# Layer norm applied to gathered rows, means and squares of attention's sums from a weight column and ScalarE, weight sums on GpSimd, and last choices of 12 and 8 tiles

## The chip, the cores and the metric

One core of one Trainium2 chip runs the whole kernel in a single launch. The metric is the device time in microseconds (us) of an execution. Times of a kernel are given as the median of several runs; a profile is one execution of its own, whose time is given beside its span.

In the profile PE is TensorE's matrix product, PEld its weight load, DVE is VectorE, ACT ScalarE, POOL GpSimd, and SP the engine that starts most transfers. L12 is line 12 of the kernel before.

## The reference, cut to what matters

The model has three blocks, each after a layer norm without gain: a mixture of experts, attention, the same mixture of experts again. x is (4, 2048, 256), so N = 8192 tokens of D = 256.

```python
x = x + 0.5 * moe(layernorm(x), router_w, wg, wu, wd)
x = x + attention(layernorm(x), Wq, bq, Wv, bv, Wo, bo)
x = x + 0.5 * moe(layernorm(x), router_w, wg, wu, wd)

def attention(x):                      # 16 heads of 16
    q, v = heads(x @ Wq + bq), heads(x @ Wv + bv)
    q = softmax(q, over the 16 columns of a head) * s
    k = softmax(q, over the tokens) * s          # keys are made of q
    return merge(q @ (k.T @ v)) @ Wo + bo

def moe(x):                            # 8 experts, F = 1024
    topw, topi = top_k(softmax(x @ router_w.T), 2)
    topw = topw / (topw.sum() + 1e-6)
    # every expert takes the 1280 tokens with the largest weights among those that chose it
    eo = (silu(rows @ wg[e]) * (rows @ wu[e])) @ wd[e]
    return scatter_add(topw * eo)
```

The layer norm is (x - mean) / sqrt(var + 1e-5) over the 256 columns. As the norm has no gain, it is one factor and one addend for each token: x * rstd + shift, with rstd = 1/sqrt(var + 1e-5) and shift = -mean * rstd.

## The kernel before, in words

The tokens are 64 tiles (T) of 128 (P). They lie in SBUF as xw, 128 x 64 x W: W = D + 2E = 272 columns (L61), of which the first 256 are the token's row of x and the 16 behind them are used for the router. Everything is float32 on TensorE. All arithmetic of PE, DVE, ACT and POOL runs on each engine in the order in which it is written (`manual_schedule`; in the stage of the experts POOL's is left out of it); the transfers that SP starts (`write_rows`, the stores of the output, the loads of weights) have an order of their own.

**First router** (`first_router`, L1178). Per quad of tiles, rows are transposed and multiplied with the router's weights, whose column means have been taken away, so that no mean of x is needed for the logits. DVE's bn_stats give mean and variance of a row in two halves; `norm_of` (L171) makes rstd and shift of them with four DVE operations, `deviation` (L165, POOL, two operations) and three more on POOL. Then `choose` (L212) finds the two best experts of every token with their renormalised weights: some twenty small DVE operations and one exp on ACT, as a generator that stops eleven times, and at the end two POOL operations that write, into the 16 columns behind a row, half the weight for each expert (L272) and whether the expert was chosen (L273). The weights also go to w.

**Route** (`route`, L278). For each expert the 1280th largest weight is found by 30 steps of bisection on the bits of a float. A step is a compare on DVE that also counts (L309), a small product on TensorE that adds the counts over the partitions (L310), and three small DVE operations, the last at L316; the next compare needs the result. Equal weights are settled after it (L322 to L336), running counts become slots (scans at L328 and L337, L338), four transposes bring them back to the order of the tokens (L343), and L345 to L353 split the slots in two parts. `next(beside, None)` (L311) lets another generator issue a few instructions in every step. In the first route that is `norm_beside` (L198): it normalises the 64 tiles in place, by turns on POOL (L194) and ACT (L196), writes them tile by tile of 16 to DRAM (`write_rows`, L275), and drives `attention_weights` (L861), which prepares the weights of attention with some small products. In the second route nothing runs beside.

**Experts** (`experts`, L452; 16 chunks of five tiles, two chunks for each expert). `RowList` (L355) makes the list of an expert's 1280 tokens by one-hot products (L413); its end, L427, yields the indices ixs (L433). `gather` (L464) fetches the rows of a chunk with an indirect DMA for each tile (L471, POOL), 272 columns wide. `blank` (L477) multiplies each row with the column that says whether the token chose this expert, since slots that no token fills hold another token's row. `turn` transposes the rows (L496), and the products follow. Gate and up products use a seven-product scheme (Strassen-Winograd): it needs sums of the weights' blocks, ws (`sums_of_w`, L507: eight DVE operations of 128 x 512 for each expert, recorded at L502) and wds (`sum_of_wd`, L520, four DVE operations), and sums of the rows' blocks (`sums_of_x`, L544). `sixth_product` (L610) ends in the DVE addition u2. Results are scaled by the token's weight (L703) and added to DRAM by indirect DMA (L704). At the start of the stage (L835 to L851) the order on DVE is: ixs, the eight sums ws of expert 0, then the odd tile's blank; in chunk 0 `sum_of_wd(0)` stands ahead of the sixth product (L635).

**Attention** (`attention`, L924). The tiles are taken two at a time (i = 0 to 31) through a software pipeline, one iteration of the loop at L1123 for each pair: `stats` (L938), `turn_x`, `project` (L957: q, and with 8 columns more the router's logits of x), `largest` (L962), `exp` (L975), `share` (L979 to L982), `keys` (L989, L991), `turn_q` (L1000), `sums` (L1012, the product of keys and x, summed over a batch element of 8 pairs). After a batch element `context_1` to `context_4` (L1021 to L1062) make the matrix that turns q into attention's output and, in 8 further columns, into its part of the next router's logits: W1 = D + E = 264 columns (L857). Then `add_y` (L1064) multiplies, and `take_y` (L1078) adds the result to the row (L1080), takes bn_stats of the two tiles (L1082), starts the store of four tiles to the output (L1085), and every second time calls `norm_of`. When 16, 16, 12, 16 and 4 tiles are complete (L1091), a `choose` is started for them, and `choose_on` (L1097) drives it: two steps in each iteration, with two `norm_row` on ACT, until the choice is through and its rows are written. The loop's tail, from L1165 on, has its own counts of steps; the last two choices run side by side from L1170 on, and their rows are normed after them (L1173).

In each iteration the written order on ACT is xs and ek of pair i-3 (`keys`), exp of pair i-2, the copies of the two transposes, and then what `choose_on` and `take_y` issue.

Of the kernel before, what the change touches and what calls it, by code (L numbers as in the profile page):

```python
# [1 line left out]

# [24 lines left out]
def macaron_kernel(  # L27
# [33 lines left out]
    W = D + 2 * E  # L61
# [128 lines left out]
    def norm_row(xw, t, gpsimd=False):  # L190

        row, by, of = xw[:, t, 0:D], rstd[:, t : t + 1], shift[:, t : t + 1]
        if gpsimd:
            nc.gpsimd.tensor_scalar(row, row, by, of, ALU.mult, ALU.add)  # L194
        else:
            nc.scalar.activation(row, row, AF.Identity, bias=of, scale=by)  # L196

    def norm_beside(xw, to, steps=iter(())):  # L198


        t, busy = 0, True
        while t < T or busy:
            busy = next(steps, 0) != 0
            for gpsimd in (True, False) if busy else (False, True, False):
                if t < T:
                    norm_row(xw, t, gpsimd)
                    t += 1
                    if t % NJ == 0:
                        write_rows(xw, to, slice(t - NJ, t))
            yield  # L210

    def choose(xw, w, ts, pool):  # L212
# [60 lines left out]
        nc.gpsimd.tensor_scalar(xw[:, ts, D + E :], by_token, 0.0, None, ALU.is_gt)  # L273
# [4 lines left out]
    def route(w, pool, ppool, beside=iter(())):  # L278
# [5 lines left out]
        def new(name):  # L284
            return pool.tile(FULL, F32, name=name)
# [17 lines left out]
        above, tie = new("above"), new("tie")  # L303
# [36 lines left out]

        ps = ppool.tile([P, GT, P], F32, tag="turn", name="back", bufs=1)
# [110 lines left out]
    def experts(name, src, dst, wait_for, weights, wpool, pool, ppool):  # L452
# [8 lines left out]
        lists, got, xTs, turned, ws, wds, xs = {}, {}, {}, {}, {}, {}, {}  # L461
# [15 lines left out]
        def blank(k, *tiles):  # L477
            for i in tiles:
                if k < len(chunks):
                    e, r = chunks[k][0], got[k][i]  # L480
                    has = r[:, D + E + e : D + E + e + 1]
                    if k == 0 and i % 2:
                        nc.vector.tensor_scalar(r[:, 0:D], r[:, 0:D], has, None, ALU.mult)
                    else:
                        nc.scalar.mul(r[:, 0:D], r[:, 0:D], has)
# [21 lines left out]
        def sums_of_w(e, m):  # L507

            if e >= E:
                return  # L510
            if m == 0:
                ws[e] = pool.tile([P, 2, 4, FH], F32, tag="ws", name="ws", bufs=1)
            v, o = weights[e][m], ws[e]
            a11, a12, a21, a22 = v[:, 0, :FH], v[:, 1, :FH], v[:, 0, FH:], v[:, 1, FH:]
            tt(o[:, m, 0, :], a21, a22, ALU.add)
            tt(o[:, m, 1, :], o[:, m, 0, :], a11, ALU.subtract)
            tt(o[:, m, 2, :], a11, a21, ALU.subtract)
            tt(o[:, m, 3, :], a12, o[:, m, 1, :], ALU.subtract)
# [40 lines left out]
        def units(k):  # L559
# [75 lines left out]
            sum_of_wd(k, 0)  # L635
            sixth_product(0)
            sum_of_wd(k, 1)
# [92 lines left out]
        def early(k, p):  # L730

            if p == 0 and more:
                lists[chunks[k][0] + 1] = more.pop(0).end()
                gather(k + 1)
            elif p == 2:
                blank(k + 1, 0, 1, 2, 3)
            elif p == 3:
                blank(k + 1, 4)
# [97 lines left out]
        with tc.manual_schedule(engines=ENGINES - {mybir.EngineType.Pool}):  # L836
# [9 lines left out]
            for m in range(2):  # L846
                sums_of_w(0, m)
            blank(0, *range(TURN))
            for q in (0, 2):
                turn(0, q)  # L850
            blank(0, *range(TURN, CH))  # L851
# [5 lines left out]
    W1 = D + E  # L857
# [3 lines left out]
    def attention_weights(pool, ppool):  # L861
# [21 lines left out]
        nc.gpsimd.tensor_copy(wqx[:, :, D:], wrx[:, :, :E])  # L883
# [20 lines left out]
        for k in range(DC):  # L904
            for c in range(DC):
                nc.tensor.matmul(
                    ps[:, k * E : (k + 1) * E], woT[:, c, k * P : (k + 1) * P], wqx[:, c, D:],
# [3 lines left out]
        nc.scalar.copy(wox[:, :, D:], ps[:, : DC * E].rearrange("p (k e) -> p k e", k=DC))  # L911
        yield
        ps = ppool.tile([P, 2 * D], F32, tag="turn", name="bor", bufs=1)
        for c in range(DC):
            bob = pool.tile([P, P], F32, tag="bob", name="bob", bufs=2)
            nc.scalar.mul(bob, ones, boT[:, c : c + 1])
            nc.tensor.matmul(ps[:, :E], bob, wqx[:, c, D:], start=(c == 0), stop=(c == DC - 1))
            yield
        nc.scalar.mul(box[:, D:], ps[:, :E], 1.0 / H)
# [4 lines left out]
    def attention(xw, w, to, weights, pool, ppool):  # L924
# [6 lines left out]
        st3 = pool.tile([P, T, 6], F32, name="st3")  # L931
# [144 lines left out]
        choosing, chosen = [], []  # L1076

        def take_y(i, ps):  # L1078
            xs = xw[:, 2 * i : 2 * i + 2, 0:W1]
            nc.vector.tensor_tensor(xs, xs, ps[:, :, 0:W1], ALU.add)  # L1080
            for t in (2 * i, 2 * i + 1):
                nc.vector.bn_stats(st3[:, t, :], xw[:, t, 0:D])  # L1082
# [3 lines left out]
            if i % 2:  # L1086
                norm_of(st3, slice(2 * i - 2, 2 * i + 2), pool)
# [3 lines left out]
            for n in (NJ, NJ, NJ - 4, NJ, 4):  # L1091
                stop += n
                if 2 * i + 2 == stop:
                    ts = slice(stop - n, stop)
                    choosing.append((ts, choose(xw, w, ts, pool), list(range(ts.start, stop))))

        def choose_on(n, m, which=0):  # L1097

            while len(choosing) > which and n:
                ts, steps, tiles = choosing[which]  # L1100
                while n:
                    n -= 1
                    if next(steps, 0) == 0:
                        steps = None
                        break
                if steps is None and ts.stop > T - NJ:
                    chosen.append(choosing.pop(which))
                    continue
                for t in tiles[: m if steps else None]:
                    norm_row(xw, t)  # L1110
                del tiles[:m]
                if steps is None:
# [7 lines left out]
        with tc.manual_schedule(engines=ENGINES):  # L1120
            stay_busy(ppool.tile([P, 2, 2 * D], F32, tag="py", name="py", bufs=1)[:, 0, :], 7)
            stats(0, 2)
            for i in range(LAST):  # L1123
# [6 lines left out]
                if b3 == B - 1:  # L1130
                    choose_on(1, 0)
# [192 lines left out]
```

## Time and profile before

| | |
|---|---|
| median of three runs | 1992.24 us (1991.15 to 1992.62) |
| the profiled execution's own time | 1991.06 us |
| its span | 1989.1 us |
| mean granted TensorE clock | 0.959 |
| busy PE | 1831.6 us (92%), 8756 products |
| busy PEld | 1332.4 us |
| busy DVE, ACT, POOL | 1401.2, 957.6, 1019.5 us |
| moved by DMA | 147.66 MB |

The span divides into stages, by the times of their first and last instructions:

| stage | us |
|---|---|
| first router and its choice | 0 to 49 |
| first route, bisection from 50.6 to 90.7 | 49 to 103 |
| list of expert 0, gather, start of the products | 103 to 127 |
| experts | 127 to 895 |
| attention, with the choices for the second experts | 895 to 1136 |
| second route, list and start | 1136 to 1213 |
| experts | 1213 to 1989 |

The lines shown in the prediction are of two kinds. A stretch has its bounds (A:B), its length, and then the busy time of PE, PEld, DVE, ACT and POOL with the number of instructions that began in it, the granted clock as a share of full speed, the busy share of the DMA engines, and GB/s. A line of the instructions in order of time has start, duration, engine, line, operation, result and operands with their shapes; in brackets stands how long the engine was idle before it, and what ended that.

### The profile page before, as it was taken

To read this page: it belongs to the slowest core of one execution; us is meant where nothing else is said; L and a number is where in the kernel's file an instruction comes from. 1 tells how busy PE (TensorE), PEld (TensorE's weight loads), DVE (VectorE), ACT (ScalarE), POOL (GpSimd) and SP (SyncE) were. 2 spreads that over 40 slices of the span, in tenths; PEclk is the share of its full clock that TensorE was granted. 3 is DMA by queue.
4 is the path that set the end of the run, shared out by engine and by line. 5 is a ranking of instruction groups with operands and counts; after the bars stand their busy time and mean duration, and the time that the engine had idled before them with its cause. 6 is when DMAs were issued, how large, how long until landed. Compare 5 with 4: busy or idle time off the path is not lost.

```text
span 1989.1 us, 25375 instructions
## 1 busy us (share of the span) xinstructions
PE 1831.6 (92%) x8756; PEld 1332.4 (67%) x8756; DVE 1401.2 (70%) x2555; ACT 957.6 (48%) x2371; POOL 1019.5 (51%) x1017
## 2 busy tenths in 40 slices
PE   6379999999999999999999627999999999999997
PEld 5247777777777777777887415777777777777776
DVE  7866767676767676647788886676767676676763
ACT  5435454554546463325565405554646363737332
POOL 4435555555555555535555304555555555555552
PEclk8589999999999999999999858999999999999999
DMA  9911313222222221125002531222222222231121
GB/s 357 309 29 28 91 31 88 58 61 71 49 70 49 71 49 28 28 24 172 33 33 88 191 135 29 67 52 71 49 70 49 70 49 75 44 94 29 31 29 19
DMA packets 99935, 147.66 MB, mean 74 GB/s; under 512 B 7512, under 2 KB 86368, under 8 KB 99680
## 3 DMA queue, kind: packets, MB, share of 16 engines
q1 hardware_dynamic: 69072, 102.77, 15.2%
q0 software_dynamic: 30720, 43.27, 13.4%
q8 instruction: 69, 1.13, 0.2%
q14 instruction: 58, 0.48, 0.1%
q10 hardware_dynamic: 16, 0.01, 0.0%
HBM read 98.84 MB, written 55.57 MB: 78 GB/s over the span
## 4 chain that ended last, share of the span: by engine, by line
PE 82%; DVE 8%; issue 1%; POOL 1%; ACT 1%; DMA 1%; POOLq 0%; DVEq 0%; ACTq 0%; SPq 0%
PE mm L570 48%; PE mm L770 23%; PE tr L496 2%; PE back L722 2%; PE qp L957 1%; PE pc L1012 1%; PE ix L413 1%; PE py L1070 1%; DVE above L309 1%; PE mm L828 1%; DVE st L1082 1%; DVE xw L1080 1%; DVE q L965 1%; DVE m L970 0%; DVE z L979 0%
## 5 line engine op out<-in xcount | busy, mean ns | idle before, releaser
L570 PE MATMUL mm<-xs,ws 128*128 128x320 f32 x1536 | 476.9, 433 | 3.9 <-DVE u L502 3.0
L505 POOL TENSOR_TENSOR ct<-ct 128x320 f32<-128x320 f32 x360 | 338.8, 941 | 190.2 <-DVE ct L601 166.7
L570 PEld LDWEIGHTS mm<-xs,ws 128*128 128x128 f32 x1536 | 284.3, 190 | 113.0 <-DVE u L502 4.1
L502 DVE TENSOR_TENSOR ct<-u,mm 128x640 f32<-128x640 f32 x256 | 209.8, 819 | 180.1 <-PE mm L570 169.0
L502 DVE TENSOR_TENSOR ct<-ct,mm 128x640 f32<-128x640 f32 x288 | 235.8, 819 | 74.6 <-PE mm L570 74.1
L598 ACT ACTIVATE ct<-ct 128x960 f32<-128x960 f32 (+2 forms) x192 | 141.7, 738 | 298.7 <-DVE ct L502 298.7
L471 POOL DMA_INDIRECT r<-rows,ixs x160 | 157.6, 985 | 235.9 <-ACT eo L703 172.8
L770 PE MATMUL mm<-ct,wds 128*128 128x320 f32 x960 | 278.5, 433 | 0.0
L407 ACT ACTIVATE lo<-from_below,behind_lo 128x129 f16<-128x129 f32 x896 | 272.9, 395 | 0.0
L770 PEld LDWEIGHTS mm<-ct,wds 128*128 128x128 f32 x960 | 178.5, 190 | 73.2 <-DVE ct L502 6.4
L770 PE MATMUL mm<-ct,wdt 128*128 128x320 f32 x720 | 213.5, 433 | 0.0
L704 POOL DMA_INDIRECT acc<-eo,ixs x80 | 127.7, 1596 | 141.9 <-ACT eo L703 124.0
L704 POOL DMA_INDIRECT out_dram<-eo,ixs x80 | 127.6, 1596 | 141.9 <-ACT eo L703 124.0
L570 PE MATMUL mm<-xsT,wgt 128*128 128x320 f32 x512 | 183.5, 440 | 0.0
L570 PE MATMUL mm<-xsT,wut 128*128 128x320 f32 x512 | 180.7, 435 | 0.0
L601 DVE TENSOR_TENSOR ct<-ct 128x640 f32<-128x640 f32 (+1 forms) x128 | 166.0, 1297 | 18.8 <-ACT ct L598 18.8
L502 DVE TENSOR_TENSOR u<-p,mm 128x640 f32<-128x640 f32 x128 | 105.0, 821 | 88.3 <-PE mm L570 80.6
L770 PEld LDWEIGHTS mm<-ct,wdt 128*128 128x128 f32 x720 | 132.1, 190 | 47.5
L607 ACT COPY p<-mm 128x640 f32<-128x640 f32 x128 | 88.3, 690 | 154.3 <-PE mm L570 154.3
L570 PE MATMUL mm<-xsT,ws 128*128 128x320 f32 x512 | 158.7, 432 | 0.0
L703 ACT ACTIVATE eo<-back,r 128x256 f32<-128x256 f32 x150 | 65.0, 478 | 152.7 <-PE back L722 152.7
L570 PEld LDWEIGHTS mm<-xsT,wut 128*128 128x128 f32 x512 | 97.7, 191 | 40.7 <-issue 0.8
(226 smaller groups left out, 2820.0 us busy)
## 6 DMA issues: line engine op xcount, KB each, us to landing
wgt<-in_L_ffn_wg_dram SPq DMA_DIRECT2D x16, 1024.0 KB, 5.0
wut<-in_L_ffn_wu_dram SPq DMA_DIRECT2D x16, 1024.0 KB, 7.5
wdt<-in_L_ffn_wd_dram SPq DMA_DIRECT2D x16, 1024.0 KB, 5.3
rows<-xw SPq DMA_DIRECT2D x7, 2176.0 KB, 15.0
xw<-in_L_attn_x_dram SPq DMA_DIRECT2D x16, 512.0 KB, 8.4
out_dram<-xw SPq DMA_DIRECT2D x16, 512.0 KB, 2.9
xw<-acc SPq DMA_DIRECT2D x15, 512.0 KB, 8.8
r<-rows,ixs POOLq DMA_INDIRECT x160, 2.8
```

Source lines behind the costliest of these rows:

```text
L407: nc.scalar.activation(lo[:, t, :], from_below, AF.Sign, bias=at, scale=1.0)
L471: nc.gpsimd.indirect_dma_start(out=r, out_offset=None, in_=src[:, :], in_offset=bass.IndirectOffsetOnAxis(ap=lists[e][:, i : i + 1], axis=0),)
L496: nc.tensor.transpose(ps[:, (i - i0) * P : (i - i0 + 1) * P], got[k][i][:, c * P : (c + 1) * P], ident)
L502: nc.vector.tensor_tensor(o, a, b, op)
L505: nc.gpsimd.tensor_tensor(o, a, b, op)
L570: nc.tensor.matmul(ps, a, b, start=start, stop=True, skip_group_check=not start)
L598: nc.scalar.activation(h(p)[:, qs, :], h(p)[:, qs, :], AF.Silu)
L601: engine.tensor_tensor(h(p)[:, qs, :], h(p)[:, qs, :], hT(p)[:, qs, :], ALU.mult)
L607: nc.scalar.copy(p1, ps)
L703: nc.scalar.mul(eo, ps, got[k][i][:, D + e : D + e + 1])
L704: ins = nc.gpsimd.indirect_dma_start(out=dst[:, :], out_offset=bass.IndirectOffsetOnAxis(ap=lists[e][:, i0 + i : i0 + i + 1], axis=0), in_ ...
L770: nc.tensor.matmul(ps, a(p), b(p), start=(p == 0 and not more), stop=(p == NF - 1), skip_group_check=more)
```

## The change

- Rows are written to DRAM as they are, right after their choice. `norm_row` and `norm_beside` are gone. A row grows by 8 columns (W = D + 3E = 280): behind the half weights stand, for each expert, a factor, (chosen) x rstd, and an addend, (chosen) x shift. `choose` ends with four POOL operations in place of two. In the experts, `norm` takes the place of `blank`: row x factor + addend, with both read from the gathered row; the tiles are split between ACT and DVE as before.
- The eight sums ws of expert 0 are made on POOL, issued one by one beside the bisection of each route (in the first, ahead of the steps of `attention_weights`). Those of later experts stay on DVE. ws moves to the pool of the weights.
- In the route, above and tie become float16; fourteen products of 128 columns, whose result is not used (`stay_busy`, L157), stand ahead of the four transposes.
- In chunk 0, `sum_of_wd(0)` stands behind the sixth product.
- W1 = D + E + 1: one further column of the weights, with -1/D in the part that x is multiplied with, makes attention's projection and output yield minus the mean of each row. `take_y` has no bn_stats: ACT squares (row - mean) and adds up along the row (accum_out), `deviation` makes rstd from the sum, and one POOL operation makes shift.
- The choices are of 16, 16, 12, 12 and 8 tiles. `choose_on` only takes steps and writes rows; the counts of its steps in the loop's tail change.

```diff
-    W = D + 2 * E
+    W = D + 3 * E
...
         nc.gpsimd.tensor_scalar(xw[:, ts, D : D + E], by_token, 0.5, None, ALU.mult)
-        nc.gpsimd.tensor_scalar(xw[:, ts, D + E :], by_token, 0.0, None, ALU.is_gt)
+        factor, by = (xw[:, ts, D + k * E : D + (k + 1) * E] for k in (1, 2))
+        nc.gpsimd.tensor_scalar(factor, by_token, 0.0, None, ALU.is_gt)
+        nc.gpsimd.tensor_tensor(by, factor, tok(shift[:, ts]), ALU.mult)
+        nc.gpsimd.tensor_tensor(factor, factor, tok(rstd[:, ts]), ALU.mult)
...
-        above, tie = new("above"), new("tie")
+        above, tie = new("above", F16), new("tie", F16)
...
+        stay_busy(ppool.tile([P, GT, P], F32, tag="turn", name="turn", bufs=1)[:, 0, :], 14, P)
         ps = ppool.tile([P, GT, P], F32, tag="turn", name="back", bufs=1)
...
+    def weight_sums(engine, e, wpool, weights, ws, *which):
...
+                engine.tensor_tensor(o[:, m, to, :], a, b, op)
+                yield
...
-        def blank(k, *tiles):
+        def norm(k, *tiles):
...
-                    has = r[:, D + E + e : D + E + e + 1]
+                    row = r[:, 0:D]
+                    by, of = (r[:, D + j * E + e : D + j * E + e + 1] for j in (1, 2))
                     if k == 0 and i % 2:
-                        nc.vector.tensor_scalar(r[:, 0:D], r[:, 0:D], has, None, ALU.mult)
+                        nc.vector.tensor_scalar(row, row, by, of, ALU.mult, ALU.add)
                     else:
-                        nc.scalar.mul(r[:, 0:D], r[:, 0:D], has)
+                        nc.scalar.activation(row, row, AF.Identity, bias=of, scale=by)
...
-            sum_of_wd(k, 0)
+            if k > 0:
+                sum_of_wd(k, 0)
             sixth_product(0)
+            if k == 0:
+                sum_of_wd(k, 0)
             sum_of_wd(k, 1)
...
-            for m in range(2):
-                sums_of_w(0, m)
-            blank(0, *range(TURN))
+            norm(0, *range(TURN))
...
-    W1 = D + E
+    W1 = D + E + 1
...
-        nc.gpsimd.tensor_copy(wqx[:, :, D:], wrx[:, :, :E])
+        nc.gpsimd.tensor_copy(wqx[:, :, D : D + E], wrx[:, :, :E])
+        nc.gpsimd.memset(wqx[:, :, D + E :], -1.0 / D)
...
             nc.vector.tensor_tensor(xs, xs, ps[:, :, 0:W1], ALU.add)
             for t in (2 * i, 2 * i + 1):
-                nc.vector.bn_stats(st3[:, t, :], xw[:, t, 0:D])
+                square = pool.tile([P, D], F32, tag="square", name="square", bufs=2)
+                nc.scalar.activation(
+                    square, xw[:, t, 0:D], AF.Square, bias=xw[:, t, W1 - 1 : W1], accum_out=squares[:, t : t + 1]
+                )
...
             if i % 2:
-                norm_of(st3, slice(2 * i - 2, 2 * i + 2), pool)
+                ts = slice(2 * i - 2, 2 * i + 2)
+                deviation(squares[:, ts], 4, pool, rstd[:, ts], 1.0 / D)
+                nc.gpsimd.tensor_tensor(shift[:, ts], xw[:, ts, W1 - 1], rstd[:, ts], ALU.mult)
...
-            for n in (NJ, NJ, NJ - 4, NJ, 4):
+            for n in (NJ, NJ, NJ - 4, NJ - 4, 8):
...
-                    choose_on(2, 2)
+                    choose_on(2)
...
-                    choose_on({LAST - 3: 0, LAST - 2: 5, LAST - 1: 3}.get(i, 4), 0)
+                    choose_on({LAST - 5: 0}.get(i, 4))
             while choosing:
                 for k in reversed(range(len(choosing))):
-                    choose_on(1, 0, k)
-            for ts, _, tiles in chosen:
-                for t in tiles:
-                    norm_row(xw, t)
-                write_rows(xw, to, ts)
+                    choose_on(1, k)
...
-                steps = norm_beside(xw, rows[0], steps)
+                for b in range(B):
+                    write_rows(xw, rows[0], slice(b * NJ, (b + 1) * NJ))
+                steps = chain(weight_sums(nc.gpsimd, 0, wpool, weights, ws, 0, 1), steps)
                 route(w, pool, ppool, steps)
...
-                route(w, pool, ppool)
+                route(w, pool, ppool, weight_sums(nc.gpsimd, 0, wpool, weights, ws, 0, 1))
```

## The prediction

> **What bounds the kernel now.** I read the stages first (busy time by stretch), then the chain that ended last, then the order of instructions around the places where that chain leaves TensorE. Stretches, with the busy time of PE, PEld, DVE, ACT and POOL, then the granted clock:
>
> ```profile
> 49.00:91.00 42.00, 14.56 (x88) 10.69 (x87) 35.76 (x153) 19.97 (x43) 21.67 (x33) 0.50 1.04 333
> 103.00:127.00 24.00, 13.14 (x88) 7.37 (x81) 14.20 (x27) 6.33 (x17) 10.19 (x10) 0.74 0.23 58
> 127.00:895.00 768.00, 767.43 (x3460) 546.38 (x3459) 523.25 (x723) 383.01 (x978) 411.56 (x346) 1.00 0.24 52
> 895.00:1136.00 241.00, 216.23 (x1100) 183.06 (x1098) 198.04 (x605) 126.19 (x257) 130.18 (x221) 0.98 0.30 96
> 1136.00:1213.00 77.00, 20.92 (x157) 12.78 (x157) 59.79 (x199) 12.92 (x31) 11.49 (x13) 0.56 0.41 137
> 1213.00:1989.10 776.10, 765.83 (x3455) 545.79 (x3455) 523.60 (x724) 383.00 (x978) 411.45 (x346) 1.00 0.24 51
> ```
>
> The two expert stages are 1544 us of solid TensorE; nothing there can give. What the change can move lies in the rest: the two routes with the way into their experts, and attention. The order of instructions at the first experts' start:
>
> ```profile
> 108.66 0.17 DVE L433 CAST ixs<-ixf 128x16 int32<-128x16 f32 x1
> ...
> 109.93 1.37 POOL L471 DMA_INDIRECT r<-rows,ixs  x1 [9.66 <-DVE ws L502]
> ...
> 113.09 1.02 POOL L471 DMA_INDIRECT r<-rows,ixs  x1 [0.30 <-issue]
> ...
> 118.16 0.95 POOL L471 DMA_INDIRECT r<-rows,ixs  x1 [0.30 <-issue]
> ```
>
> The list of rows (ixs) is ready at 108.83, yet the first gather starts 1.10 later and lasts 1.37, while DVE forms the weight sums ws from 108.75 to 113.88. Later gathers last 0.95. In attention, one iteration of the middle (project to project 6.17, as at 1012.92, 1019.09, 1025.27, with PE never idle):
>
> ```profile
> 1016.65 0.69 DVE L979 TENSOR_REDUCE z<-q 128x32 f32<-128x512 f32 x1
> ...
> 1018.46 0.90 ACT L989 ACTIVATE xs<-xw,rstd 128x256 f32<-128x256 f32 x2
> 1018.67 0.40 DVE L229 SCALAR_TENSOR_TENSOR tmp<-ex,rev 128x128 f32<-128x128 f32 x1
> 1019.26 0.62 ACT L991 ACTIVATE ek<-q 128x512 f32<-128x512 f32 x1
> 1019.78 0.62 ACT L975 ACTIVATE q<-q 128x512 f32<-128x512 f32 x1
> 1019.83 0.69 DVE L1080 TENSOR_TENSOR xw<-xw,py 128x528 f32<-128x528 f32 x1
> 1020.56 0.75 DVE L1082 BATCH_NORM_STATS2 st<-xw 128x6 f32<-128x256 f32 x2
> ```
>
> The chain names DVE here, but PE has no gap: the two engines are level, and DVE's 11.36 busy us of 12.00 (1010 to 1022) hang over nothing. So DVE time saved is not span saved. ACT is in order too: xs, ek and exp (L989, L991, L975), and today none of it waits for the add of L1080.
>
> **Experts' start (twice).** The eight ws sums leave DVE for POOL beside the bisection. There POOL is busy 21.7 of 42 us in the first route and idle in the second; the 26 row norms that leave POOL (14.0 us) are more than the eight sums. At 1.06 to 1.27 us each (rows L972, L891, same width) they take 9 to 10 us and are over long before 99.65 and 1186.8, when POOL is wanted; their weights have landed by then (issued at 20 and 1136, 5 to 29 us to land). Without cover they would stall TensorE's small products of the attention weights, and with them the bisection; they need not end before about 73, by my count of the steps, and end near 66.
> The gather then starts 0.30 after ixs (the gap that every later one shows) and lasts 0.95: the third, which the chain runs through, starts at 111.63 and not 113.09: -1.46; in the second stage 1198.79 and not 1200.26: -1.47. [...] Ends: 0 and -1.5.
> sum_of_wd(0) moved behind the sixth product takes its 0.60 off the chain (wds sits between ct at 124.47 and u at 125.81); PE's next products cover it afterwards. The norm in place of blank has a second pointer: 588 ns (L196) for 509 (L485), +0.08 once on the chain. In the chunks the four of them grow by 0.32 before an ACT gap of 1.34 (386.36 to 387.70), the fifth by 0.08 before one of 1.18: nothing. Rows of 1120 for 1088 bytes add 3% to writes that today end at 97 with the gather at 110, and are now issued earlier: nothing. Sum -1.98 a stage, **-3.9**.
>
> **Route (twice).** Fewer bytes for above and tie touch one row only: L336 with all operands f16, 0.69 to about 0.42 (L382 does 1024 such in 0.684). The accumulating compares have one f32 input and stay at 0.746. stay_busy(14): 28 passes of 128 columns, about 0.22 cold and 0.11 warm (L1046: 8 in 0.91); after a pause TensorE warms in 3.7 us here (py at 1108.73: 8 in 3.70, then 1.78). Start 92.3, warm at 96.0, end 97.2, about when St is done; the four transposes then take 0.6 instead of 1.10. Together -0.5 a route; ends -0.9 (warm early) and +0.9 (not warm in time). **-1.0**. Choose gets two more POOL operations, before POOL's free time. The row norms removed from ACT were on no chain.
>
> **Attention, the loop.** bn_stats (0.75 for two) and norm_of (0.57 for every second iteration) leave DVE: about 1.0 of DVE in each iteration, worth nothing while PE is the bound. Squares of the new sums join ACT behind the add, and in front of the next iteration's xs, ek and exp; behind exp wait z (L979), the statistics, choose and the next add. That is a new round trip. From the rows, start to start: z to end of add 2.71 plus the choose operations c between; two squares; xs 0.80, ek 0.51, exp 0.61; hops 0.08. A square: 0.43 apart (L485, four in 1.71) plus its accumulator's read. No ACT row shows one: ends 0 and 0.18 (the smallest ACT rows); the nearest is DVE's read, 0.085. So two squares 1.03, ends 0.86 and 1.4 (if the read also waits for the pipe). Round trip 5.74 + c against PE's 6.17: hidden without choose, not with it.
> First choice (six iterations, c = 0.97, 1.16, 1.35, 0.72, 1.2, 0.66): 40.5 - 37.0 = 3.5 over. PE feels it only once exp ends later than 5.0 after its project (ek must precede sums at 4.44, xT the next project), and it ends at 3.5 now: 1.5 is slack, **+2.0** is stall. Second choice, the three iterations that still have statistics: 20.7 - 18.5 - 1.5 = **+0.7**. Contexts: g (L1025) queues behind two squares: +0.2 and +0.5. End of the loop, counted from the last project (1085.35): add 19 ends at 2.0 (now 1.5), exp at 5.1, z and choose, add 20 at 8.2 (8.0), exp at 11.2 (8.3), add 21 at 14.3 (11.7), its squares, xs, ek at 16.9, last sums and rc at 18.7 (15.8): **+2.9**, since in these short iterations nothing else covers the trip. Sum **+6.3**; ends +3.3 and +11.4 for the two ends of a square.
>
> **Attention, the tail.**
>
> ```profile
> 1128.20 0.64 DVE L1080 TENSOR_TENSOR xw<-xw,py 128x528 f32<-128x528 f32 x1
> ...
> 1135.59 0.21 DVE L226 TENSOR_TENSOR w<-p,rs 128x32 f32<-128x32 f32 x1
> ```
>
> From 1108.73 (first sum of the last eight) the last add ends 20.1 later, the last w 27.1. Now PE gives one in about 1.85 after 3.7 for the cold first. The choice of 12 starts after the fifth add, waits for its deviation (squares, then 1.3 on POOL, of which the power at L169 takes 1.05) and for its exp behind squares; with 0.69 an add and 3.9 of choose the last add ends near 19.5. Squares 1.1; POOL has the 12 tiles' factors first (four operations, 2.0), then 1.3 of deviation: 22.3. A choice of 8 alone is about 4.3 (four tiles took 4.1 with the other's operations between): 26.6. **-0.5**; ends -3 (POOL free, exp not queued) and +1.5.
>
> **The numbers.** -3.9 - 1.0 + 6.3 - 0.5 = +0.9. Against the profiled execution (span 1989.1, 1991.06 with what lies around it) 1992.0; that execution is 1.2 below the median of 1992.24, so **1993.1**. Below 0.2%, about 4 us, a measurement of this kernel can tell nothing from no change.
>
> **Rivals.** (1) *Gains are paid back in the loop*, as above: 0.45, 1989 to 1997. (2) *The round trip stays under PE's period*, because choose shrinks without POOL in its way: then PE's idle 1.25 and 2.31 in two contexts give about 1, the loop's end nothing, the tail 1 to 3: -2.5, so -7.4 in all, **1985**, 0.28. For it: DVE loses 1.0 per iteration; against it: those operations were behind the add, not in the trip. (3) *Slower: ScalarE's accumulator.* One mechanism: the read waits until the square is through, 0.7 per square, two squares 1.4: loop +11.4, total +6.5, **1998.8**, 0.24. It costs about 14 us per us of the pair, so it decides from 1.25 a pair (0.63 each) on. For it: every ACT row has some 0.2 of fixed time. Against it: DVE's read overlaps its instruction's end. (4) *Square is not in exp's table.* [...] Today Silu, Sign and copies share a table (four loads in all): 0.03, near 2040.
>
> Range 1984.5 to 1999. Faster 0.29, same 0.43, slower 0.28.
>
> **What would show it.** First gather within 0.4 us of ixs and 0.95 long (else 1.5 a stage is missing); L336 near 0.42; the back transposes in about half the time; project-to-project 6.17 where no choice is made and 6.5 or more in the later choose iterations, with xs waiting for squares and PE's sums for ek; squares 0.5 apart; rc some 3 us later after the last project; expert stages unchanged. Wrong if the choose iterations stay at 6.17 (rival 2), or the pair of squares takes over 1.25 (rival 3).

## The result and the profile after

| | before | changed |
|---|---|---|
| median | 1992.13 us (1989.15 to 1992.76, 7 runs) | 1997.93 us (1995.96 to 2000.41, 7 runs) |
| ratio to the kernel before | | 1.0035, 95% interval 1.0025 to 1.0044 |
| profiled execution, its span | 1991.06, 1989.1 us | 2000.41, 1998.7 us |
| busy DVE, ACT, POOL | 1401.2, 957.6, 1019.5 us | 1354.7, 953.9, 1026.4 us |

The changed kernel is slower by 0.35% by the ratio, which is 7 us; the two medians lie 5.8 apart. The profiled execution of it was the slowest of its seven, 2.5 above the median, and that of the kernel before lies 1.1 below its median, so the stages below add up to more. The prediction was 1993.1, a gain or loss too small to see (0.43). It gave 0.28 to a slower kernel.

Below, every stage of the profiled execution is set beside the one before. The bounds are taken at the same instructions in both: the end of the list of rows (ixs), the start of the second block of products with ws (from there TensorE is steady), the first projection, rc of the last context (the reciprocal with which a context begins on DVE), and the last w. St are the slots that the four transposes at the end of a route bring back to the order of the tokens.

| stage | before | after | difference | predicted |
|---|---|---|---|---|
| start to bisection | 50.55 | 50.44 | -0.1 | 0 |
| bisection to ixs, first | 58.28 | 59.21 | +0.9 | -0.5 |
| ixs to steady products, first | 17.76 | 16.23 | -1.5 | -2.0 |
| experts, to the first projection | 774.66 | 776.29 | **+1.6** | 0 |
| projections to rc of the last context | 199.90 | 209.20 | **+9.3** | +6.3 |
| rc to the last w | 34.65 | 33.88 | -0.8 | -0.5 |
| last w to ixs, second | 60.19 | 60.29 | +0.1 | -0.5 |
| ixs to steady products, second | 17.11 | 15.97 | -1.1 | -2.0 |
| experts, to the end | 776.00 | 777.19 | **+1.2** | 0 |
| sum | | | **+9.6** | +0.9 |

The same stages as stretches, with the columns of the prediction's first view (bounds, length, busy PE, PEld, DVE, ACT, POOL, granted clock, DMA share, GB/s):

```profile
125.88:895.90 770.02, 769.46 (x3461) 546.62 (x3462) 521.98 (x724) 390.17 (x978) 412.43 (x346) 1.00 0.24 52
895.90:1145.40 249.50, 222.50 (x1099) 184.36 (x1097) 165.91 (x477) 132.74 (x334) 126.58 (x197) 0.97 0.30 99
1221.50:1998.70 777.20, 767.31 (x3455) 545.48 (x3455) 522.18 (x724) 390.20 (x978) 412.39 (x346) 1.00 0.24 52
```

In attention DVE has lost 32 of its 198 us, as intended, and the stretch is longer. In the experts ACT has 7 us more, and TensorE, full from end to end, still needs longer for the same products.

**The loop of attention.** One iteration of the first choice in the changed kernel, 1035.24 to 1041.75 from project to project (6.51, where it was 6.17):

```profile
1036.65 0.70 DVE L1073 TENSOR_TENSOR xw<-xw,py 128x530 f32<-128x530 f32 x1
...
1037.44 0.51 ACT L1076 ACTIVATE square<-xw 128x256 f32<-128x256 f32 x1 [2.62 <-DVE xw L1073]
1037.86 0.19 ACT L1076 ACTIVATION_READ_ACCUMULATOR square<-xw 128x1 f32 x1
...
1038.44 0.89 ACT L982 ACTIVATE xs<-xw,rstd 128x256 f32<-128x256 f32 x2
1039.24 0.61 ACT L984 ACTIVATE ek<-q 128x512 f32<-128x512 f32 x1
1039.91 2.00 PE L1005 MATMUL pc<-xs,ek 128*128 128x257 f32 x8
1040.41 0.69 DVE L972 TENSOR_REDUCE z<-q 128x32 f32<-128x512 f32 x1 [1.42 <-ACT q L968]
```

ACT idles 2.62 until the add is there, then does the two squares, and only then xs and ek, for which TensorE's sums and, through exp, DVE's z wait. ACT and DVE idle by turns: no engine is full, and the round trip sets the time. The pair of squares takes 1.00 (1037.44 to 1038.44), the accumulator's read overlaps its neighbours and costs about 0.09 of it. The iterations with a choice take 6.29, 6.74, 6.51, 6.53 and 6.44, those without 6.19.

**The experts.** ScalarE in the third quarter of an expert's first chunk: the norms of four gathered tiles, eight Signs for the next list, then the copy p1. The changed kernel:

```profile
335.56 2.08 ACT L485 ACTIVATE r<-r 128x256 f32<-128x256 f32 x4
337.54 2.45 ACT L390 ACTIVATE lo<-from_below,behind_lo 128x129 f16<-128x129 f32 x8
339.88 0.68 ACT L598 COPY p<-mm 128x640 f32<-128x640 f32 x1
```

The same place before the change:

```profile
335.86 1.71 ACT L485 ACTIVATE r<-r 128x256 f32<-128x256 f32 x4
337.47 2.44 ACT L407 ACTIVATE lo<-from_below,behind_lo 128x129 f16<-128x129 f32 x8
339.81 0.68 ACT L607 COPY p<-mm 128x640 f32<-128x640 f32 x1
```

From the first norm to the copy it is 3.95 before and 4.32 after. TensorE adds its second product onto the bank that this copy reads. It had 0.16 in hand, and now stops for 0.21 in each such chunk, at no other place: of the instructions of an expert, all starts agree to 0.01 up to this one, and all behind it are 0.21 late. One expert lasts 96.45 for 96.24. Seven experts in each stage have such a chunk.

**The route.** TensorE in the first route of the changed kernel:

```profile
92.07 6.28 PE L161 MATMUL turn<-row_of_ones,ident 128*128 128x128 f32 x28
...
98.41 0.66 PE L326 MATMUL back<-ident,St 128*128 128x128 f32 x4
```

A product is two passes here, and a pass took 0.22. The granted clock rose at 98.18, when the last of the 28 was under way, and St had been ready since 96.70. The transposes themselves did become short, 0.66 for 1.08, and L336 took 0.43 for 0.69, as predicted. So St was there 0.25 earlier, the transposes took 0.42 less, but they began 1.72 after St where it had been 0.15: +0.9 in all.

**The start.** The first gathers of the changed kernel, with nothing on DVE:

```profile
109.47 0.18 DVE L416 CAST ixs<-ixf 128x16 int32<-128x16 f32 x1
110.73 1.25 POOL L470 DMA_INDIRECT r<-rows,ixs  x1 [9.69 <-issue]
112.28 0.96 POOL L470 DMA_INDIRECT r<-rows,ixs  x1 [0.30 <-issue]
113.55 0.95 POOL L470 DMA_INDIRECT r<-rows,ixs  x1 [0.30 <-issue]
```

The first one still starts 1.08 after ixs (0.82 in the second stage), and still lasts longer than the others. It wasn't ws that kept it from starting.

### The profile page after: what moved, and what is told of

It reads as the page before. It is cut to its first block, busy times and chain, and to the rows that moved or that the text cites. A ratio compares the mean times of both kernels' runs of the same rounds, so it can differ in the third digit from the quotient of the medians.

```text
span 1998.7 us, 25360 instructions
## 1 busy us (share of the span) xinstructions
PE 1852.3 (93%) x8812; PEld 1344.5 (67%) x8812; DVE 1354.7 (68%) x2411; ACT 953.9 (48%) x2397; POOL 1026.4 (51%) x988
## 3 DMA queue, kind: packets, MB, share of 16 engines
q8 instruction: 70, 1.15, 0.2%
## 4 chain that ended last, share of the span: by engine, by line
PE 83%; DVE 6%; ACT 3%; issue 1%; POOL 1%; DMA 1%; POOLq 0%; ACTq 0%; DVEq 0%; SPq 0%
PE mm L561 48%; PE mm L764 23%; PE tr L496 2%; PE qp L950 2%; PE back L716 2%; PE pc L1005 2%; PE py L1063 1%; PE ix L396 1%; DVE above L291 1%; PE mm L822 1%; ACT square L1076 1%; ACT xs L982 1%; DVE xw L1073 1%; DVE z L972 1%; DVE cand L298 0%
## 5 line engine op out<-in xcount | busy, mean ns | idle before, releaser
L592 DVE TENSOR_TENSOR ct<-ct 128x640 f32<-128x640 f32 (+1 forms) x128 | 161.0, 1258 | 21.7 <-ACT ct L589 21.7
```

Source lines behind the costliest of these rows:

```text
L592: engine.tensor_tensor(h(p)[:, qs, :], h(p)[:, qs, :], hT(p)[:, qs, :], ALU.mult)
```

## The experiments

Eleven kernels ran, in three groups, each beside the kernel before. On the chip of the third group (the last three) the kernel before took 1996.34 us, in the first two 1991.04 and 1991.97. So ratios to the kernel before are compared, and 0.0005 of a ratio is 1 us. The changed kernel stands at 1.0035, and its own interval is 1 us to each side. So e4, e5 and e6 can't be told from it by their times alone; what is said of them rests on their traces.

| kernel | ratio | 95% interval | against the changed kernel |
|---|---|---|---|
| e1_bn_dve | 1.0012 | 1.0003 to 1.0022 | -4.6 us |
| e2_late | 0.9983 | 0.9974 to 0.9992 | -10.4 |
| e3_norm_split | 1.0016 | 1.0007 to 1.0025 | -3.8 |
| e4_busy8 | 1.0026 | 1.0016 to 1.0037 | -1.8 |
| e5_ws_dve | 1.0043 | 1.0030 to 1.0057 | +1.6 |
| e6_ctx | 1.0031 | 1.0020 to 1.0042 | -0.8 |
| e7_best | 0.9968 | 0.9956 to 0.9981 | -13.4 |
| e8_best_w | 0.9959 | 0.9945 to 0.9972 | -15.2 |
| e9_three | 1.0088 | 1.0072 to 1.0103 | +10.6 |
| e10_16_4 | 0.9959 | 0.9946 to 0.9973 | -15.2 |
| e11_busy0 | 0.9967 | 0.9956 to 0.9978 | -13.6 |

**e1_bn_dve: squares off ScalarE.**

```diff
-                nc.scalar.activation(square, xw[:, t, 0:D], AF.Square, ..., accum_out=squares[:, t : t + 1])
+                nc.vector.bn_stats(st3[:, t, :], xw[:, t, 0:D])
...
-                deviation(squares[:, ts], 4, pool, rstd[:, ts], 1.0 / D)
+                norm_of(st3, slice(2 * i - 2, 2 * i + 2), pool)
```

> The changed kernel with one part undone: take_y has DVE's bn_stats and norm_of again in place of ScalarE's squares; the further weight column, the choices of 12 and 8, norms at the gather, ws on GpSimd stay. Theory (squares in the round trip of ScalarE and VectorE stretch attention): the project-to-project times of the choice iterations return to 6.19, the last project to rc to 15.8, and the total falls by 5 to 8 us from 1997.9, to 1990 to 1993. Lower end if TensorE's clock dips in the two contexts (3.3 us of the profiled execution) go with the squares, upper end if they are chance. Rival (the loop is longer because of the wider rows and the four operations at the end of a choice): no change, 1997 to 1998.

Measured: 1993.7 us, 4.6 less by the ratio, just short of the 5 to 8 expected. All iterations of the loop without a context last 6.19 or 6.20, and the last project to rc takes 15.61. So the squares made the stalls, and the 265th column costs no more than 0.02 an iteration. The first context still lasts 10.9, where no square has been done yet: that part isn't theirs. At the tail this kernel is 0.9 longer than before (rc to the last w 35.50), though the tail before had 3.4 us of halved clock, from 1108.7 on, and this one none: without the relief of DVE the choices of 12 and 8 gain nothing.

**e2_late: the same squares, an iteration later.** A pair's squares, deviation and choice are issued just ahead of the next pair's add, behind that iteration's xs, ek, exp and copies, as long as the loop has projections or keys to do.

```diff
+                if i < NP + 3:
+                    if has(y - 1):
+                        square_y(y - 1)
                 if has(y):
                     take_y(y, ps)
+                if i == NP + 3:
+                    square_y(y - 1)
+                if i >= NP + 3:
+                    square_y(y)
```

> The changed kernel with the squares of a pair issued one iteration later, behind the next iteration's xs, ek, exp and the two copies, so that they stand in front of nothing that DVE waits for; same instructions, same counts. Theory (it is the round trip add, squares, xs, ek, exp, z, add that stalls TensorE, not ScalarE's load): stalls of 1.5 in the first choice, 0.65 in the second and most of 2.7 at the loop's end vanish, total 4 to 5 us less than 1997.9, about 1993.5; the choices start an iteration later, which may give back up to 1. Rival (ScalarE has too much work there, whatever its order): no change.

Measured: 1987.15 us, 10.4 less than the changed kernel and 3.4 less than the kernel before (interval 1.6 to 5.2). One iteration earlier than the one above (6.74 in the changed kernel), in this kernel's trace:

```profile
1025.64 0.70 DVE L1073 TENSOR_TENSOR xw<-xw,py 128x530 f32<-128x530 f32 x1
...
1028.32 0.52 ACT L1081 ACTIVATE square<-xw 128x256 f32<-128x256 f32 x1
...
1029.31 0.90 ACT L982 ACTIVATE xs<-xw,rstd 128x256 f32<-128x256 f32 x2
```

The squares stand behind the copies, ahead of an xs that has time, and no iteration without a context is over 6.20. It is the place of the squares in ScalarE's order that made the loop slow, not their number. The gain is twice what was expected for two reasons. The relief of DVE now pays where PE does wait: the second and third contexts take 9.06 and 9.59 (9.66 and 10.72 before the change), the last project to rc 14.70 (15.80). And the changed kernel's third context had a stretch of slow clock (see e6), which is gone here. From the first projection to rc it is 197.6, where it was 199.9 before and 209.2 in the changed kernel.

**e9_three: one square more.**

```diff
-            for t in (2 * i, 2 * i + 1):
+            for t in (2 * i, 2 * i, 2 * i + 1):
```

> The changed kernel with one square more for each pair (the first tile's is done twice; the result is the same). Theory (round trip): a third square of 0.50 lengthens add, squares, xs, ek, exp, z, add to about 6.7 plus the choice's operations, over TensorE's 6.19 in every iteration with an add and statistics: the steps of the choice iterations go from 6.3 to 6.7 up to 6.8 to 7.2, those without a choice to 6.3 or more, the last project to rc from 18.5 to 20; total +5 to +8, near 2004. Rival (the squares cost only by ScalarE's load, and it has 3 us to spare in each iteration): +1 at most.

Measured: 2013.64 us on a slower chip, 10.6 more than the changed kernel by the ratio. That is more than the +5 to +8 expected. The choice iterations take 7.58, 7.39, 7.15, 7.19 and 7.08, so each grows by 0.64 or more; those without a choice stay at 6.19, against the expectation; the last project to rc takes 20.42. The second context fell into the slow clock here too, of which more below; that is some 1.7 of the 10.6. The other 8.9 are about 18 us per us of the pair, more than the "about 14" of the prediction.

**e3_norm_split: the fourth norm moved.**

```diff
-                norm(k + 1, 0, 1, 2, 3)
+                norm(k + 1, 0, 1, 2)
             elif p == 3:
-                norm(k + 1, 4)
+                norm(k + 1, 3, 4)
```

> The changed kernel with the fourth gathered tile's norm moved from the third quarter of a chunk (ahead of eight Signs and the copy p1) to the last, beside the fifth tile's. Theory (four norms of 0.52 instead of 0.43 push the copy p1 of every first chunk of an expert late by 0.37, of which 0.16 is slack): TensorE's pause of 0.21 in each of 14 such chunks goes, -2.9 us, about 1995.0; one expert lasts 96.24 again. Rival (TensorE itself is slower by 0.2% in this execution): still 96.45 for an expert, no change.

Measured: 1994.36 us, 3.8 less. The experts' stages are 1.9 and 1.6 shorter, and the pause of 0.21 is gone: the three norms take 1.59, less than the four `blank` did:

```profile
334.53 1.59 ACT L485 ACTIVATE r<-r 128x256 f32<-128x256 f32 x3
336.02 2.44 ACT L390 ACTIVATE lo<-from_below,behind_lo 128x129 f16<-128x129 f32 x8
338.36 0.68 ACT L598 COPY p<-mm 128x640 f32<-128x640 f32 x1
```

So 2.9 of the loss came from 0.09 us more for an instruction, at a place with a slack of 0.16.

**e4_busy8: fewer idle products.**

```diff
-        stay_busy(..., 14, P)
+        stay_busy(..., 8, P)
```

> The changed kernel with 8 products instead of 14 ahead of the back transposes. Theory (28 passes take 0.22 each, end 1.65 and 1.25 after the slots St are there, and only their sheer length makes the transposes warm): the wait goes, the transposes are cold again (1.08 instead of 0.66), net -1.2 in the first route and -0.8 in the second, about 1996. Rival (the warm transposes are what counts): +0.8, 1998.7.

Measured: 1996.06 us, 1.8 less. The second route became 1.2 shorter, the first (bisection to ixs) only 0.1, though its slots were ready 1.15 earlier, counted from the start of the bisection:

```profile
98.61 0.28 DVE L335 TENSOR_SCALAR slot_lo<-slot 128x512 int16<-128x512 int16 x1
100.48 0.69 DVE L357 TENSOR_TENSOR hi<-counts,slot_hi 128x1024 f16<-128x1024 int16 x1 [1.58 <-DMA rows<-xw]
```

The list's first compare waits for the write of the rows, because its tile lies where the rows lay. That wait was hidden in the changed kernel behind the idle products. The prediction had put the write at "nothing"; here it holds the compare until about 100.4. In the changed kernel the compare starts 0.19 after the slots, so there the write itself costs nothing yet.

**e8_best_w: the write hurried** (with the three mends of e7_best, below).

```diff
+                written = [write_rows(...) for b in range(B)]
...
-        load_expert(1, wpool, weights)
+        load_expert(1, wpool, weights, written)
```

> The same three mends, and the weights of expert 1 are loaded only behind the four writes of rows in the first stage. Theory (the list of expert 0 waits for the end of the write, which shares the DMA engines with 3 MB of weights): the write ends some 9 us earlier, the first compare of the list starts when its slots are there, 1.4 earlier: 1.4 below the kernel with the three mends alone. Rival (the write is not what the list waits for): no change.

Measured: 1982.97 us, ratio 0.9959, where e7_best has 0.9968: the intervals overlap, but the trace shows the wait gone: the compare starts at 99.11, 0.19 after the slots, where it was 1.02 after them in e7_best.

**e5_ws_dve: the weight sums back on DVE.**

```diff
+            for m in range(2):
+                sums_of_w(0, m)
             norm(0, *range(TURN))
...
-                route(w, pool, ppool, weight_sums(nc.gpsimd, 0, wpool, weights, ws, 0, 1))
+                route(w, pool, ppool)
```

> The changed kernel with one part undone: expert 0's eight weight sums stand on VectorE behind the list again, in both stages, and nothing runs beside the bisection but attention's weights. The prediction's step (ws on VectorE holds the first gathers, 1.46 a stage): the first gather starts 1.1 after ixs and lasts 1.37 instead of 1.25, and the way from ixs to steady products grows by 1.5, total +3 (2001). The reading of the two profiles (the 1.1 between ixs and the first gather is there without ws too, so ws costs 0.4 on three gathers, and the odd tile's norm is held behind ws): +0.7 to 0.9 a stage, +1.6 in all, 1999.5. [...]

Measured: 1999.96 us, +1.6. The first stage in this kernel's trace:

```profile
110.62 1.37 POOL L470 DMA_INDIRECT r<-rows,ixs  x1 [10.21 <-DVE ws L448]
112.29 1.21 POOL L470 DMA_INDIRECT r<-rows,ixs  x1 [0.30 <-issue]
113.81 1.01 POOL L470 DMA_INDIRECT r<-rows,ixs  x1 [0.30 <-issue]
113.92 0.68 DVE L448 TENSOR_TENSOR ws<-wut,ws 128x512 f32<-128x512 f32 x1
115.38 0.41 DVE L483 TENSOR_SCALAR r<-r 128x256 f32<-128x256 f32 x1 [0.78 <-DMA r<-rows,ixs]
```

The gap between ixs and the first gather is 1.1 in both kernels (in the second stage 0.9 here and 0.8 in the changed kernel). The first three gathers last 1.37, 1.21 and 1.01 with ws beside them, 1.25, 0.96 and 0.95 without, so that the third starts 0.36 later after ixs, and 0.75 in the second stage. The odd tile's norm isn't held behind ws, as the expectation had it: ws is over 0.78 before it, and it waits for its gather. The way from ixs to steady products is 17.02 and 16.69 for 16.23 and 15.97. In the second stage the gathers make that difference. In the first they make half of it; TensorE's clock came back to full 13.9 after ixs here and 12.4 in the changed kernel, and the other half, 0.41, arises where it was still halved. So the move to GpSimd is worth 0.4 to 0.75 a stage, a quarter to a half of what the prediction took.

**e6_ctx: TensorE kept busy in the contexts.**

```diff
             g = parts[b]
+            if b < B - 1:
+                stay_busy(ppool.tile([P, 2, 2 * D], F32, tag="py", name="py", bufs=1)[:, 0, :], 10, P)
```

> The changed kernel with ten products of 128 columns, whose result nobody reads, ahead of the transposes in the first three contexts. Theory (TensorE idles 1.4 to 2.4 there, and its clock is halved for 3.4 us in some executions, 1.65 us each): the clock stays at 1.00, the context steps are 9.2 and 10.7 or less instead of 10.89 and 12.75, total -2 to -3.3, 1995 to 1996, with less scatter between runs. Rival (the steps are long because ScalarE and VectorE are late, the clock only follows): no gain, or +0.5 where the products themselves stand in the way.

Measured: 1997.24 us, -0.8, within the interval of no change. In the changed kernel's first context the granted clock (the column third from the right) is halved:

```profile
950.00:951.00 1.00, 0.64 (x4) 0.40 (x4) 0.96 (x3) 0.74 (x2) 1.00 (x2) 1.00 0.00 0
...
952.00:953.00 1.00, 1.00 (x6) 1.00 (x6) 0.00 (x0) 1.00 (x3) 0.88 (x2) 0.50 0.00 0
```

It falls at 951.5 and is back at 954.9; the third context has the same from 1060.7 to 1064.2. The profiled execution before the change had neither. TensorE's wait ahead of the third context's transposes, in the changed kernel and then before:

```profile
1059.98 0.66 PE L1027 MATMUL trg<-ident,g 128*128 128x128 f32 x4 [2.43 <-ACT qT L995]
1054.87 0.66 PE L1034 MATMUL trg<-ident,g 128*128 128x128 f32 x4 [2.11 <-ACT qT L1002]
```

With the fillers the clock stays at 1.00 in all three contexts, and their steps are 9.80, 10.65 and 11.08 for 10.89, 9.87 and 12.75: the dips are gone, but the fillers stand in the way (+0.8 where there was no dip). In the traces that is 2.0 less; the medians give 0.8, since not every execution of the changed kernel need have both dips. So the dip as a cost of about 1.7 is shown, and curing it by idle products doesn't pay.

The first context dips in e1, e3, e4, e5, e9 and e11 too, and not in e2, e7, e8 and e10, where the products there are the same. The traces show what decides. In each of them, all changes of the granted clock lie on a grid of 3.41 us, whose place relative to the kernel differs from one execution to the next. I counted TensorE's idle time in every interval of that grid between 905 and 1102, in all thirteen traces. In the thirteen intervals with 1.84 to 3.08 idle, the clock was halved in the next one; in those with at most 1.76 it was not. The first context idles 1.44 and 0.68 close together, so it dips if enough of both falls into one interval of the grid, and not if the grid parts them. That is chance. The third context of the kernel before idles 2.11 and 0.68 and could dip as well, as an estimate from the same figures; that of e2 idles 0.94 and could not. So that the squares made the changed kernel's dip there, with 2.43, is not shown.

**e7_best: three mends together** (e2_late, e3_norm_split, e4_busy8).

> Three mends of the changed kernel at once: squares an iteration late, the fourth tile's norm in the last quarter of a chunk, 8 idle products in the route. If the three costs are separate, their single gains add up: -10.8, -3.6, -1.9, so 1981.7. If part of them is the same wait (the first route's list also waits for the rows' write), 1983.

Measured: 1984.51 us. By the ratios -13.4, where the single gains make -16.0. The 2.6 between them are within the intervals, so whether the gains overlap stays open. The rows' write does hold the first list here (1.02), as it did in e4.

**e10_16_4 and e11_busy0: two parts of e8_best_w undone.**

```diff
-            for n in (NJ, NJ, NJ - 4, NJ - 4, 8):
+            for n in (NJ, NJ, NJ - 4, NJ, 4):
...
-                    choose_on({LAST - 5: 0}.get(i, 4))
+                    choose_on({LAST - 3: 0, LAST - 2: 5, LAST - 1: 3}.get(i, 4))
```

> The kernel with the three mends and expert 1's weights behind the rows, with the last choices of 16 and 4 tiles and their counts of steps as before the change. Theory (the choices of 12 and 8 move operations but the last choice alone is what ends the tail): 8 tiles' 23 operations of 0.22 against 4 tiles' of 0.18 among 16 tiles' of 0.29: the tail from rc to the last w within 0.5 of it, 1982.5 to 1983.5. Rival (12 and 8 are the reason for the shorter tail): +1 to +2, 1984.5.

Measured: ratio 0.9959, the same as e8_best_w. From rc to the last w it is 32.35 in e10 and 32.17 in e11, which has the choices of 12 and 8, both without a slow clock there. In this order of the squares, the sizes of the last choices make no difference.

e11_busy0 has no `stay_busy` in the route:

> The same kernel as e8_best_w without any idle products in the routes. Theory (8 products never warm the clock in time): back transposes 1.08 as with 8, no change, 1983. Rival (some of them warm the products that follow, the list's or the transposes): +0.4 to +0.9, 1983.6.

Measured: ratio 0.9967, which can't be told from e8_best_w's. From the last w to the second list's slots it is 50.51 with none and 50.50 with 8 products in e8; e7 and e10, whose 8 products did warm the clock, have 50.05. So they give 0.45 in some executions and nothing in others.

## Why the prediction was wrong, step by step

- **The loop's round trip: right, and the largest term.** First choice +1.6 (said +2.0), second +0.65 (+0.7), end of the loop +2.7 (+2.9), a pair of squares 1.00 (1.03), the add, squares, xs, ek, exp, z chain as described. e2 and e9 show it from both sides. Left out was the further column, 0.02 in 27 iterations, 0.5. The contexts were put at +0.7 and had +3.9 in the profiled execution: about 3.3 of that are the two clock dips, for which the prediction had no term.
- **The chunks: this is the step that failed most plainly.** "The four of them grow by 0.32 before an ACT gap of 1.34 (386.36 to 387.70) [...]: nothing". The gap is that of an expert's second chunk. In the first chunk the Signs of the next list fill it, and there the slack is 0.16. The price of the pointer was right (0.09 an instruction), and it cost 2.9 in 14 chunks, as e3 confirms. Both chunks had to be looked at.
- **The gathers: wrong.** "-1.46" a stage; the third gather came 0.35 and 0.74 earlier, within the prediction's ends of 0 and -1.5, and e5, which puts ws back, delays it by 0.36 and 0.75. The 1.1 between ixs and the first gather was taken for ws because ws ran beside it; the engine named as the releaser proved nothing, and it stands without ws. What ws does change is the lengths: 1.37 against 1.25 and 1.21 against 0.96 for the first two gathers (e5 and the changed kernel).
- **The route: wrong in sign** (+0.9 and +0.1 for -0.5 each). 14 products were sized by a warm-up of 3.7 us, seen once in the tail of the profile; in these routes they ran 6.28 and 5.86, and the clock rose 6.1 and 5.2 after their start. The traces show why one sighting isn't a measure: in the fourteen routes with 14 products the clock rose 2.9 to 6.1 after the first, and the products ended 0.1 to 1.7 after St.
- **The tail: right** (-0.8 for -0.5), and by DVE's relief (e1), not by the choices' sizes (e10).
- **"DVE time saved is not span saved" held only where PE is full.** At the contexts and at the loop's end it is worth 2.8 us, and e2 collects it.

So in the profiled execution +0.9 became +9.6: +2.8 in the chunks, +2.0 in the routes, +1.3 in the starts, +3.0 in the loop (dips and width, less a little on the stalls) and -0.4 in the tail and ahead of the first bisection. Without the two dips it would be about +6.3, close to the +7 of the ratio. Rival 3 named nearly the right time by a wrong mechanism: a square with its accumulator's read takes 0.50, not 0.7. Rival 2 fell in its form, since the choice iterations did not stay at 6.17; that its time (1985) is near what the same instructions reach in a better order (e2: 1987) is luck. Rival 3's sum is off: its +6.5 leaves out the tail's -0.5. The price behind rival 4's 2040 is shown by no run: the profiled execution of the changed kernel has four table loads of 1.28, as many as the one before, and none of them at the 64 squares. Neither changes the forecast.

What stays open: what fills the 1.1 between ixs and the first gather, and how many executions of either kernel had a dip in a context.

## What to carry to other kernels

When an engine is relieved, ask where the work lands in the *order* of the engine that takes it: a short operation that waits for late data holds everything queued behind it (ScalarE idled 2.62 in the iteration shown), and moving it behind what is ready can turn a loss into a gain (here 10 us, part of it by the clock, with not one instruction less). A "nothing" must be checked at every form of the place it stands for, since in a full pipeline 0.2 us repeated 14 times is 3 us. Idle products to warm a clock meet its grid at any place: too few of them warm nothing in some executions (8 did so in three of eight routes here), and enough of them can end after the work that they should speed up is ready (14 did, by 0.1 to 1.7).

## What the runs showed of the hardware

- The accumulator's read on ScalarE is an instruction of its own (0.19) that costs about 0.09 behind a 0.5 us activation: two tiles of 256 in 1.00. Square caused no table load: with 64 squares the profiled execution has four loads of 1.28, as many as before the change.
- A second pointer operand made a 128x256 activation 0.09 longer (four in 2.08 for 1.71), on DVE 0.06 (0.41 for 0.35).
- In each of the thirteen traces TensorE's granted clock changes only on a grid of 3.41 us, which lies differently in each. In attention it was halved for the next 3.41 after each interval with 1.84 us idle or more (13 of 13), and after none with 1.76 or less. A dip costs about 1.7 where TensorE is full (first context 10.89 for 9.23). That may be a part of the scatter between runs of these kernels: of the changed kernel's seven, the four under 1998 had a mean clock of 0.960 or 0.961, the three above 1999 one of 0.958 or 0.959. Only a profiled execution shows where it was halved.
- Indirect gathers of 128 rows were 0.1 to 0.4 longer beside 128x512 f32 tensor_tensor on VectorE (1.42 and 1.34 for 1.13 and 0.97 in the second stage), and started at most 0.1 later for it.
